# Linear layer's start placed ahead of the state space layer's tail, its norm weights applied to transposed features, and the windowed layers' dates changed

## Chip, cores and metric

One Trainium2 chip, one core. The metric is the device time of one execution in microseconds (us), as a median over runs; lower is better. A core has five engines that run their own instruction streams in order and wait for one another by semaphores: TensorE (PE, matmul and transpose, with weight loads shown as PEld), VectorE (DVE), ScalarE (ACT), GpSimd (POOL) and SyncE (SP, which issues most transfers). Matmul results land in PSUM, everything else lies in SBUF.

## What is computed

Four layers on x of 4 x 1024 tokens with 256 features, all fp32:

```python
x = x + mamba(_layernorm(x), ...)                 # state space layer, 16 states, 512 channels
x = x + experts(_layernorm(x), ...)               # 8 experts, the best one of each token
x = x + _L1_attn_ref(_layernorm(x), ...)          # linear attention and its own feed-forward
x = x + _L1_ffn_ref(_layernorm(x), ...)           # two layers of windowed attention and feed-forward

def _L1_attn_ref(x, wq, wk, wv, wo, proj, w1, b1, w2, b2, g1, beta1, g2, beta2):
    h = _ln(x, g1, beta1)                         # (x - mean) * rsqrt(var + 1e-5) * g1 + beta1
    q = _phi((h @ wq).reshape(b, s, H, DH), proj) # elu(q @ proj) + 1, 16 heads of 64
    k = _phi((h @ wk).reshape(b, s, H, DH), proj)
    v = (h @ wv).reshape(b, s, H, DH)
    ...                                           # causal: kv and ksum run over the tokens
    x = x + attn @ wo
    h2 = _ln(x, g2, beta2)
    return x + (gelu(h2 @ w1 + b1) @ w2 + b2)
```

Two norms follow one another at the linear layer: the plain one of the model and the layer's own, with weights g1 and beta1.

## The kernel before

`run()` calls three methods one after the other: `mamba` (state space layer and experts), `linear` and `local` (both windowed layers). Every instruction passes through one helper on line 98, so the profile shows L98 everywhere and instructions are told apart by their tiles. A scheduler decides the order on each engine: where `nc.hold` is set an instruction keeps its place in program order, elsewhere it is free to move. Tokens are worked in groups of 512 (`G` = 4 blocks of 128 partitions), eight in all.

`mamba` (line 271) has a main loop over 256 steps (subsequence and state), held in program order. Behind it `nc.hold` is off, and there follow the last `output` (transposes py and acc, summed in PSUM), `finish` (the gated product, po with w_out), the experts still left (`rest`) and the last subsequence's `experts`. An experts step normalizes, computes router logits (PE's pl), on POOL and DVE the weights of the chosen expert (lg, w, cw), transposes them on PE (pcw, from cw) and runs eight experts' products (pe, from w_e, high and low halves of each fp32 operand apart: names in h and l).

`linear` (line 838) opens its pools, loads the feature projection pj, and has these parts. `weights(o)` multiplies wq and wk by pj for eight heads (PE's pf from a tile raw that a DMA on SP's queue fills) and splits the result and wv into high (ACT) and low (DVE; POOL for wv). `norm(n)` loads group n's tokens z (group 0, z0, on POOL's queue) and applies the plain norm. `project(n)` runs `features`: statistics, rstd on POOL, then for each half of the group hn = (z - mean) * rs on DVE, times the row g1 and plus the row beta1 on POOL, four transposes on PE into PSUM (pt, tag p5, three buffers shared with pf), and a split of pt into hth (ACT) and htl (DVE). Then follow the projections pq and pv. `rows` holds g1, beta1 and b2 spread over all partitions by transfers on ACT's queue.

The streams `ahead` (project) and `behind` (forward, the feed-forward) are advanced step by step in a loop over units (group, half of the heads, block) with scores (pa, masked to am), values (po, at), turn (transposes to oth, otl) and add (pw with l_wo, added to z). What is left of `behind` goes to `local`, which runs it between the first windowed group's steps.

`local` (line 1233) places its steps by dates written out as constants: a place is 10 times a tile's number plus an offset. BEHIND holds the offsets of the linear layer's leftover steps, REST the point at which that layer's buffers are freed for the windowed layers' weights, EARLY, ELOAD, EPAIR, ETURN and HOLD the steps of the first groups, TABLES and W1G0 those of weights.

The part of `features` that the change touches:

```python
for name, op in affine:
    nc.gpsimd.tensor_tensor(
        hn, hn, rows[name].unsqueeze(1).to_broadcast([P, 2, D]), op
    )
yield
pt = ps.tile([P, 2, 2 * P], F32, tag="p5", name="pt")
```

Of the kernel before, what the change touches and what calls it, by code (L numbers as in the profile page):

```python
# [9 lines left out]
F32 = mybir.dt.float32  # L10
F32R = mybir.dt.float32r
AF = mybir.ActivationFunctionType
ALU = mybir.AluOpType
AX = mybir.AxisListType
PSUM = bass.MemoryType.PSUM
DRAM = bass.MemoryType.DRAM

P = 128
D = 256
NB = 4  # L20
# [3 lines left out]
G = 4  # L24
# [13 lines left out]
HP3 = H3 // 2  # L38
FF = 1024
NF = FF // P  # L40
VW = 65
# [83 lines left out]
class Kernel:  # L125
# [142 lines left out]

    def mamba(self, xs):

        tc, ins = self.tc, self.ins
        nc = self.nc
        T, NQ = 2 * P, 2
        NSUB = NB * L // T
        SEQ = L // T
        LATER = (7, 8, 9, 10, 11, 12, 13, 14, 15)
        with ExitStack() as es:
            def pool(name, bufs, **kw):  # L280
                return es.enter_context(tc.tile_pool(name=name, bufs=bufs, **kw))

            early = pool("m_a", 1)
            mid = pool("m_f", 1)
            wp = pool("m_w", 1)
            wk = pool("m", 1)
            dp = pool("m_d", 3, space=DRAM)

            ps_d = pool("m_pd", 1, space=PSUM)
            ps_h = pool("m_ph", 2, space=PSUM)  # L290
            ps = pool("m_ps", 3, space=PSUM)

            st = [{} for _ in range(NSUB)]

# [470 lines left out]
            for s in range(NSUB):  # L765
# [10 lines left out]
                if s > 0:  # L776
                    e = experts(s - 1)
# [23 lines left out]
            for k in range(K):  # L801
# [24 lines left out]
                        now()  # L826
                tokens_first(k)
            nc.hold = False
            for t in range(2):
                output(K - 1, t)  # L830
            run(finish(NSUB - 1))
# [6 lines left out]
    def linear(self, xs, ys):  # L838


        nc, tc, ins = self.nc, self.tc, self.ins
        late, kept = ExitStack(), ExitStack()
        with ExitStack() as es:
# [4 lines left out]

            wp = pool("l_w", 1)
            st = wf = pool("l_f", 1)  # L850


            wa = pool("l_a", 1)
            wo_ = pool("l_o", 1)
            wz = pool("l_z", 1, late, side="right")
            wb = pool("l_b", 1, late, side="right")
            wl = pool("l_w2", 1, late, side="right")
            ps = pool("l_ps", 3, kept, space=PSUM)
            ps_t = pool("l_pt", 1, space=PSUM)
            ps_a = pool("l_pa", 1, space=PSUM)  # L860
            ps_o = pool("l_po", 2, space=PSUM)

            NG = 2 * NB
            ctx = [{} for _ in range(NG)]
# [14 lines left out]
            def weights(o):  # L879
# [23 lines left out]
                    raw = self.raw(st, tag="e", bufs=2, src=ins["l_wv"][k * P : (k + 1) * P, at])  # L903
                    self.split(wv[:, k, at], raw, nc.gpsimd)


            keep = wz.tile([P, P], F32, name="keep")
            nc.gpsimd.memset(keep, 1.0)
            nc.gpsimd.affine_select(
                out=keep, in_=keep, compare_op=ALU.is_ge, fill=0.0, base=0,  # L910
                pattern=[[1, P]], channel_multiplier=-1,
            )

            kv = wz.tile([P, HP3, 2, VW], F32, name="kv")
            nc.gpsimd.memset(kv, 0.0)

            def features(pool, z, dst, affine=(), **kw):

                st_ = pool.tile([P, G, 6], F32, name="fst", bufs=2)
                mv = pool.tile([P, G, 2], F32, name="fmv", bufs=2)  # L920
                for t in range(G):
                    nc.vector.bn_stats(st_[:, t, :], z[:, t, :])
                    nc.vector.bn_aggr(mv[:, t, :], st_[:, t, :])
                rs = self.rstd(pool, mv, G)
                for t in range(0, G, 2):
                    hn = pool.tile([P, 2, D], F32, name="hn", **kw)
                    for j in range(2):
                        nc.vector.tensor_scalar(
                            hn[:, j, :], z[:, t + j, :], mv[:, t + j, 0:1], rs[:, t + j : t + j + 1],
                            ALU.subtract, ALU.mult,  # L930
                        )
                    for name, op in affine:
                        nc.gpsimd.tensor_tensor(
                            hn, hn, rows[name].unsqueeze(1).to_broadcast([P, 2, D]), op
                        )
                    yield
                    pt = ps.tile([P, 2, 2 * P], F32, tag="p5", name="pt")
                    for k in range(2):
                        for j in range(2):
                            nc.tensor.transpose(  # L940
                                pt[:, k, j * P : (j + 1) * P], hn[:, j, k * P : (k + 1) * P],
                                self.ident,
                            )
                    yield
                    self.split(dst[:, :, t * P : (t + 2) * P], pt)

            def split_tile(pool, name):
# [14 lines left out]
            def project(n):  # L962
                ht = split_tile(wf, "ht")
                yield from features(
                    wf, ctx[n]["z"], ht, (("g1", ALU.mult), ("beta1", ALU.add)), tag="e", bufs=2
                )
                for o in range(2):
                    if n == 0 and o == 1:
                        weights(1)
                    qt, kt, vs = [], [], []  # L970
                    ctx[n]["heads"].append((qt, kt, vs))
                    for hp in range(4):
                        at = slice((4 * o + hp) * P, (4 * o + hp + 1) * P)
                        for name, w, dst in (("q", wq, qt), ("k", wk_, kt)):
                            pq = ps.tile([P, GT], F32, tag="p5", name="pq")
                            self.mm3(pq, [(w[:, k, at], ht[:, k, :]) for k in range(2)])
                            yield

                            e = wf.tile([P, GT], F32, name="e", bufs=2)
                            nc.scalar.activation(e, pq, AF.Exp)  # L980
                            nc.vector.tensor_scalar(e, e, 1.0, None, ALU.min)
                            s = wa.tile([P, GT], F32, name=name + "t", bufs=7)
                            nc.vector.scalar_tensor_tensor(s, pq, 0.0, e, ALU.max, ALU.add)
                            dst.append(s)
                    for t in range(G):
                        tok = slice(t * P, (t + 1) * P)
                        pv = ps.tile([P, GT], F32, tag="p5", name="pv")
                        self.mm3(
                            pv,
                            [(ht[:, k, tok], wv[:, k, o * 512 : (o + 1) * 512]) for k in range(2)],  # L990
                        )
                        yield

                        v_ = wa.tile([P, 8, VW], F32, name="va", bufs=3)
                        nc.gpsimd.memset(v_[:, :, 64:65], 1.0)
                        nc.scalar.copy(v_[:, :, 0:64], pv.rearrange("p (h e) -> p h e", e=64))
                        vs.append(v_)
                if n + 1 < NG:
                    norm(n + 1)
                yield  # L1000
# [184 lines left out]
            def stream(f):  # L1185
                for n in range(NG):
                    yield from f(n)

            norm(0)
            weights(0)  # L1190
            rows = {n: self.row(wf, n, D) for n in ("g1", "beta1")}
            rows["b2"] = self.row(wz, "b2", D)
            ahead, behind = stream(project), stream(forward)
            made = [0, 0]
            count = 4 + NF + NF // 2 * (2) + 1

            def projected(unit):
# [28 lines left out]
                        if lag <= i < len(units) + lag:  # L1226
                            f(*units[i - lag])
            run(ahead)
        return behind, late, kept, ps

    def local(self, xs, behind, late, kept, ps):
# [3 lines left out]
        with kept, ExitStack() as es:  # L1237
# [129 lines left out]
            def w2_part(l, c):  # L1367
# [16 lines left out]
            ADD_LAST = (7, 12)  # L1384
            LOAD = (1, 10, 15, 16)
            FORWARD = (4, 5, 7, 7, 7, 9, 9, 19, 19, 21, 21, 21, 23, 25, 26, 29, 32, 36, 38, 39, 45, 46, 61)
            FIRST = (-6, 2, 5, 6, 6, 9, 14)
            LOAD_FIRST = (4, 10, 16, 17)
            W1G0 = (15, 20, 18, 19)
            W1V0 = (25, 30, 28, 31)  # L1390
            W20 = (37, 41, 44, 46, 47, 52)
            QKV = (4, 6, 7, 8, 11, 12)
# [1 line left out]
            W1G = (37, 39, 40, 45)  # L1394
            W1V = (45, 50, 55, 60)
            W2 = (57, 68, 74, 77, 78, 86)
            ELOAD, EPAIR, ETURN, REST, HOLD = (-62, -60, -60, -58), (-44, -16), (-29, -13), -5, -2
            TABLES, O0 = (-42, -24, 8, 23, 32, 39), (-2, 6, 6, 8)
            EARLY = (
                (-44, -42, -42, -36, -34, -33, -33),  # L1400
                (-39, -33, -28, -28, -28, -28, -21),
                (-29, -15, -15, -15, -12, -7, 2),
                (-20, -4, -4, -1, 4, 9, 13),
            )
            BEHIND = (
                -51, -50, -47, -47, -47, -46, -40, -37, -35, -31, -31, -30, -24, -24, -18, -15,
                -14, -13, -12, -7, -1, 5,
            )


# [475 lines left out]
    def run(self, phases=("mamba", "linear", "local")):  # L1886
        nc, tc = self.nc, self.tc
        with ExitStack() as es:
            cp = es.enter_context(tc.tile_pool(name="const", bufs=1))
            dp = es.enter_context(tc.tile_pool(name="dram", bufs=1, space=DRAM))  # L1890
            self.constants(cp)
            xs = [dp.tile([P, G, D], F32, name=f"xs{i}") for i in range(2 * NB)]
            if "mamba" in phases:
                self.mamba(xs)
            if "linear" in phases:
                ys = [dp.tile([P, G, D], F32, name=f"ls{i}") for i in range(2 * NB)]
                left = self.linear(xs, ys)
                xs = ys
            if phases[-1] == "local":
                self.local(xs, *left)  # L1900
            else:
# [109 lines left out]
```

## Time and profile before

| | value |
|---|---|
| runs | 3405.77, 3407.74, 3413.19 us; median 3407.74 |
| profiled execution, its own time | 3408.97 us |
| its span, granted clock | 3407.3 us, 0.968 |
| PE busy | 3105.7 us (91%) |
| DVE busy | 2590.5 us (76%) |
| ACT busy | 2050.5 us (60%) |
| POOL busy | 1939.0 us (57%) |
| instructions | 59830 |

Times in the profile count from the first instruction. The state space layer's loop ends near 1129; from there to 1236 its tail and the start of the linear layer overlap; the linear layer runs to about 2100, a seam to the windowed layers to about 2260, and those to the end at 3407. In a view by windows each engine has its busy time and, behind the x, the number of its instructions; PEclk is the granted TensorE clock as a share of full speed. In a list of waits "PE a <- POOL b" says that PE stood before an instruction writing a until POOL had made b. In an order of time the bracket gives the idle time of the engine just before, and what ended it.

### The profile page before, as it was taken

To read this page: it belongs to the slowest core of one execution; us is meant where nothing else is said; L and a number is where in the kernel's file an instruction comes from. 1 tells how busy PE (TensorE), PEld (TensorE's weight loads), DVE (VectorE), ACT (ScalarE), POOL (GpSimd) and SP (SyncE) were. 2 spreads that over 40 slices of the span, in tenths; PEclk is the share of its full clock that TensorE was granted. 3 is DMA by queue.
4 is the path that set the end of the run, shared out by engine and by line. 5 is a ranking of instruction groups with operands and counts; after the bars stand their busy time and mean duration, and the time that the engine had idled before them with its cause. 6 is when DMAs were issued, how large, how long until landed. Compare 5 with 4: busy or idle time off the path is not lost.

```text
span 3407.3 us, 59830 instructions
## 1 busy us (share of the span) xinstructions
PE 3105.7 (91%) x21872; PEld 2639.4 (77%) x21872; DVE 2590.5 (76%) x5796; ACT 2050.5 (60%) x4082; POOL 1939.0 (57%) x2301
## 2 busy tenths in 40 slices
PE   5788888888887899999999999899999999999998
PEld 4666667666766788898888888778888888888886
DVE  6899999999999576667766766677777677777663
ACT  7777777777775232433343434676666777666664
POOL 5988888888788321001101103677677766767671
PEclk8799999999999899999999999899999999999998
DMA  2011111111110110000000002211111111111111
GB/s 92 32 44 38 36 39 46 38 36 40 41 35 29 54 63 4 1 13 20 20 7 13 19 7 77 72 32 37 48 48 49 60 40 56 47 38 46 38 41 35
DMA packets 83973, 130.60 MB, mean 38 GB/s; under 512 B 10080, under 2 KB 58016, under 8 KB 83680
## 3 DMA queue, kind: packets, MB, share of 16 engines
q1 hardware_dynamic: 81216, 124.68, 11.4%
q8 instruction: 174, 2.85, 0.3%
q10 hardware_dynamic: 2320, 1.57, 0.2%
q14 instruction: 119, 0.97, 0.1%
q0 software_dynamic: 144, 0.52, 0.0%
HBM read 99.21 MB, written 27.53 MB: 37 GB/s over the span
## 4 chain that ended last, share of the span: by engine, by line
PE 63%; DVE 16%; POOL 7%; ACT 7%; issue 6%; DMA 1%; POOLq 0%; SPq 0%; DVEq 0%; ACTq 0%
PE pq L98 10%; PE pw L98 10%; PE po L98 8%; PE pa L98 7%; PE pt L98 6%; DVE hs L98 6%; POOL hs L98 3%; PE pe L98 3%; PE pf L98 3%; PE ph L98 3%; PE pp L98 2%; PE py L98 2%; PE pv L98 2%; ACT gl L98 2%; DVE acc L98 2%
## 5 line engine op out<-in xcount | busy, mean ns | idle before, releaser
L98 POOL TENSOR_TENSOR hs<-uc,bn 128x1024 f32<-128x1024 f32 x256 | 608.7, 2378 | 67.0 <-PE ph L98 53.3
L98 DVE TENSOR_TENSOR_SCAN hs<-da,hs 128x512 f32<-128x512 f32 x512 | 608.3, 1209 | 25.2 <-POOL hs L98 12.4
L98 PE MATMUL ph<-ident,hs 128*128 128x128 f32 x2048 | 336.7, 297 | 131.7 <-DVE hs L98 66.4
L98 ACT ACTIVATE da<-dt,a 128x510 f32<-128x510 f32 x512 | 346.8, 687 | 141.7 <-DVE hs L98 135.5
L98 PEld LDWEIGHTS ph<-ident,hs 128*128 128x128 f32 x2048 | 242.6, 149 | 225.6 <-DVE hs L98 78.1
L98 POOL MEMSET va<- 128x8 f32 x64 | 7.5, 120 | 578.5 <-PE pk L98 461.5
L98 POOL TENSOR_TENSOR u<-u,ro 128x512 f32<-128x512 f32 x128 | 175.5, 1371 | 246.0 <-DVE ro L98 199.4
L98 ACT ACTIVATE sm<-sm,mx 128x256 f32<-128x256 f32 (+1 forms) x512 | 248.5, 488 | 97.6 <-DVE mx L98 96.6
L98 PE MATMUL pq<-wqkvh,yt 128*128 128x512 f32 x768 | 287.0, 415 | 0.7 <-ACT yt L98 0.7
L98 POOL TENSOR_SCALAR sm<-sm,sums 128x256 f32<-128x256 f32 (+1 forms) x512 | 237.1, 481 | 81.1 <-DVE sums L98 75.8
L98 ACT ACT_TABLE_LOAD x146 | 187.3, 1283 | 59.7 <-DVE gl L98 31.9
L98 ACT ACTIVATE term<-ph,ct 128x512 f32<-128x512 f32 x288 | 181.4, 682 | 56.6 <-PE ph L98 56.5
L98 DVE CUSTOM_DVE_ANT_0 sm<-pp,band 128x256 f32<-128x256 f32 (+1 forms) x512 | 177.8, 403 | 42.6 <-PE pp L98 42.1
L98 POOL TENSOR_TENSOR ss<-ss,power 128x16 f32<-128x16 f32 x64 | 187.7, 2932 | 5.3
L98 ACT ACTIVATE e<-pq 128x512 f32<-128x512 f32 x128 | 75.8, 597 | 184.4 <-PE pq L98 172.9
L98 PEld LDWEIGHTS pq<-wqkvh,yt 128*128 128x128 f32 x768 | 144.3, 188 | 38.2 <-issue 9.6
L98 ACT ACTIVATE sq<-pq 128x512 f32<-128x512 f32 x128 | 76.6, 599 | 142.2 <-DVE ro L98 105.1
L98 DVE SCALAR_TENSOR_TENSOR acc<-ph,ct,acc 128x512 f32<-128x512 f32 x192 | 139.7, 728 | 17.4 <-PE ph L98 17.4
L98 PE MATMUL pq<-wqkvl,yt 128*128 128x512 f32 x384 | 152.0, 396 | 0.0
L98 PE MATMUL pa<-fh,w1h 128*128 128x512 f32 x320 | 134.3, 420 | 19.1 <-ACT v L98 15.7
L98 PE MATMUL py<-ident,term 128*128 128x128 f32 x1152 | 149.1, 279 | 0.0
L98 PE MATMUL po<-va,am 128*128 128x65 f32 x1024 | 146.8, 261 | 0.0
(325 smaller groups left out, 10252.7 us busy)
## 6 DMA issues: line engine op xcount, KB each, us to landing
bn<-bd SPq DMA_DIRECT2D x64, 512.0 KB
tab<-tab SPq DMA_DIRECT2D x64, 128.0 KB
line<-yg SPq DMA_DIRECT2D x64, 128.0 KB
hn<-line SPq DMA_DIRECT2D x64, 128.0 KB
xr<-in_x SPq DMA_DIRECT2D x16, 256.0 KB
xs<-xr SPq DMA_DIRECT2D x16, 256.0 KB
hn<-xs SPq DMA_DIRECT2D x16, 256.0 KB
ls<-hn SPq DMA_DIRECT2D x16, 256.0 KB
```

Of the source, the lines that this page charges most:

```text
L98: now = f(*args, **kw)
```

## The change

Three parts.

1. `mamba` takes the generator `linear`. Its pools m_a and m_pd (a PSUM pool) are closed behind the main loop, the others move to the other side of the memory, and then `linear` runs up to its first `yield`: pools l_w, l_f and l_ps, pj, the constant keep, the cleared sums kv, `norm(0)`, `weights(0)` and four steps of `project(0)`, which are both halves' normalization and transposes. In program order all this now lies ahead of the last `output`, `finish` and the experts. The other pools of `linear` are opened behind the `yield`.
2. The rows g1 and beta1 and the 32 POOL products with them are gone. The transposed features have one feature per partition, so weights are now two scalars per partition: 32 DVE instructions, two to each pt, in place in PSUM.
3. `local` has other dates.

```diff
-    def mamba(self, xs):
+    def mamba(self, xs, then):
...
+        first = ExitStack()
...
-            early = pool("m_a", 1)
-            mid = pool("m_f", 1)
-            wp = pool("m_w", 1)
-            wk = pool("m", 1)
+            early = pool("m_a", 1, first)
+            ps_d = pool("m_pd", 1, first, space=PSUM)
+            wk = pool("m", 1, side="right")
+            wp = pool("m_w", 1, side="right")
+            mid = pool("m_f", 1, side="right")
...
             nc.hold = False
+            first.close()
+            next(then)
             for t in range(2):
                 output(K - 1, t)
...
-                    for name, op in affine:
-                        nc.gpsimd.tensor_tensor(
-                            hn, hn, rows[name].unsqueeze(1).to_broadcast([P, 2, D]), op
-                        )
                     yield
...
+                    if affine:
+                        for k in range(2):
+                            nc.vector.tensor_scalar(
+                                pt[:, k, :], pt[:, k, :], self.v("g1", k), self.v("beta1", k),
+                                ALU.mult, ALU.add,
+                            )
                     self.split(dst[:, :, t * P : (t + 2) * P], pt)
...
             norm(0)
             weights(0)
-            rows = {n: self.row(wf, n, D) for n in ("g1", "beta1")}
-            rows["b2"] = self.row(wz, "b2", D)
+            rows = {}
             ahead, behind = stream(project), stream(forward)
             made = [0, 0]
+            for _ in range(4):
+                made[0] += 1
+                next(ahead)
+            yield
...
-            FIRST = (-6, 2, 5, 6, 6, 9, 14)
+            FIRST = (-5, 2, 3, 4, 6, 7, 14)
-            W1G0 = (15, 20, 18, 19)
+            W1G0 = (16, 22, 20, 19)
-            ELOAD, EPAIR, ETURN, REST, HOLD = (-62, -60, -60, -58), (-44, -16), (-29, -13), -5, -2
-            TABLES, O0 = (-42, -24, 8, 23, 32, 39), (-2, 6, 6, 8)
+            ELOAD, EPAIR, ETURN, REST, HOLD = (-68, -58, -56, -51), (-46, -20), (-23, -12), -10, -3
+            TABLES, O0 = (-41, -22, 11, 23, 34, 39), (-2, 6, 6, 8)
...
             BEHIND = (
-                -51, -50, -47, -47, -47, -46, -40, -37, -35, -31, -31, -30, -24, -24, -18, -15,
-                -14, -13, -12, -7, -1, 5,
+                -61, -60, -54, -54, -54, -52, -47, -42, -32, -31, -28, -26, -23, -22, -20, -18,
+                -15, -14, -12, -7, 6, 8,
             )
...
             xs = [dp.tile([P, G, D], F32, name=f"xs{i}") for i in range(2 * NB)]
+            ys = [dp.tile([P, G, D], F32, name=f"ls{i}") for i in range(2 * NB)]
+            linear = self.linear(xs, ys)
             if "mamba" in phases:
-                self.mamba(xs)
...
+                self.mamba(xs, linear)
```

The four lists of EARLY change as well, each offset by up to 5 places.

More of the change, by code (lines that the diff above doesn't have):

```diff
@@ L278, in mamba, with pool @@
         LATER = (7, 8, 9, 10, 11, 12, 13, 14, 15)
+        first = ExitStack()
         with ExitStack() as es:
-            def pool(name, bufs, **kw):
-                return es.enter_context(tc.tile_pool(name=name, bufs=bufs, **kw))
-            early = pool("m_a", 1)
-            mid = pool("m_f", 1)
-            wp = pool("m_w", 1)
-            wk = pool("m", 1)
+            def pool(name, bufs, to=es, **kw):
+                return to.enter_context(tc.tile_pool(name=name, bufs=bufs, **kw))
+            early = pool("m_a", 1, first)
[3 more added lines that the diff above has]
+            mid = pool("m_f", 1, side="right")
             dp = pool("m_d", 3, space=DRAM)
-            ps_d = pool("m_pd", 1, space=PSUM)
-            ps_h = pool("m_ph", 2, space=PSUM)
-            ps = pool("m_ps", 3, space=PSUM)
+            ps_h = pool("m_ph", 2, space=PSUM, side="right")
+            ps = pool("m_ps", 3, space=PSUM, side="right")
             st = [{} for _ in range(NSUB)]
@@ L850, in linear @@
             st = wf = pool("l_f", 1)
[L853 to L857, printed above, removed]
             ps = pool("l_ps", 3, kept, space=PSUM)
-            ps_t = pool("l_pt", 1, space=PSUM)
-            ps_a = pool("l_pa", 1, space=PSUM)
-            ps_o = pool("l_po", 2, space=PSUM)
             NG = 2 * NB
@@ L904, in weights, with features @@
                     self.split(wv[:, k, at], raw, nc.gpsimd)
[L907 to L911, printed above, removed]
-            )
-            kv = wz.tile([P, HP3, 2, VW], F32, name="kv")
-            nc.gpsimd.memset(kv, 0.0)
-            def features(pool, z, dst, affine=(), **kw):
+            def features(pool, z, dst, affine=False, **kw):
                 st_ = pool.tile([P, G, 6], F32, name="fst", bufs=2)
@@ L931, in features @@
                         )
-                    for name, op in affine:
-                        nc.gpsimd.tensor_tensor(
-                            hn, hn, rows[name].unsqueeze(1).to_broadcast([P, 2, D]), op
-                        )
                     yield
@@ L964, in project @@
                 yield from features(
-                    wf, ctx[n]["z"], ht, (("g1", ALU.mult), ("beta1", ALU.add)), tag="e", bufs=2
+                    wf, ctx[n]["z"], ht, affine=True, tag="e", bufs=2
                 )
@@ L1187, in stream @@
                     yield from f(n)
+            keep = wf.tile([P, P], F32, name="keep")
+            nc.gpsimd.memset(keep, 1.0)
+            nc.gpsimd.affine_select(
+                out=keep, in_=keep, compare_op=ALU.is_ge, fill=0.0, base=0,
+                pattern=[[1, P]], channel_multiplier=-1,
+            )
+            kv = wf.tile([P, HP3, 2, VW], F32, name="kv")
+            nc.gpsimd.memset(kv, 0.0)
             norm(0)
             weights(0)
-            rows = {n: self.row(wf, n, D) for n in ("g1", "beta1")}
-            rows["b2"] = self.row(wz, "b2", D)
+            rows = {}
             ahead, behind = stream(project), stream(forward)
             made = [0, 0]
+            for _ in range(4):
+                made[0] += 1
+                next(ahead)
+            yield
+            wa = pool("l_a", 1)
+            wo_ = pool("l_o", 1)
+            wz = pool("l_z", 1, late, side="right")
+            wb = pool("l_b", 1, late, side="right")
+            wl = pool("l_w2", 1, late, side="right")
+            ps_t = pool("l_pt", 1, space=PSUM)
+            ps_a = pool("l_pa", 1, space=PSUM)
+            ps_o = pool("l_po", 2, space=PSUM)
+            rows["b2"] = self.row(wz, "b2", D)
             count = 4 + NF + NF // 2 * (2) + 1
@@ L1228, in linear @@
             run(ahead)
-        return behind, late, kept, ps
+        yield behind, late, kept, ps
     def local(self, xs, behind, late, kept, ps):
@@ L1396, in local @@
             W2 = (57, 68, 74, 77, 78, 86)
-            ELOAD, EPAIR, ETURN, REST, HOLD = (-62, -60, -60, -58), (-44, -16), (-29, -13), -5, -2
-            TABLES, O0 = (-42, -24, 8, 23, 32, 39), (-2, 6, 6, 8)
+            ELOAD, EPAIR, ETURN, REST, HOLD = (-68, -58, -56, -51), (-46, -20), (-23, -12), -10, -3
+            TABLES, O0 = (-41, -22, 11, 23, 34, 39), (-2, 6, 6, 8)
             EARLY = (
[L1400 to L1403, printed above, removed]
+                (-45, -44, -43, -37, -37, -35, -33),
+                (-36, -35, -30, -26, -26, -26, -17),
+                (-34, -18, -15, -15, -11, -7, 4),
+                (-18, -7, -2, 1, 7, 12, 15),
             )
             BEHIND = (
-                -51, -50, -47, -47, -47, -46, -40, -37, -35, -31, -31, -30, -24, -24, -18, -15,
-                -14, -13, -12, -7, -1, 5,
+                -61, -60, -54, -54, -54, -52, -47, -42, -32, -31, -28, -26, -23, -22, -20, -18,
+                -15, -14, -12, -7, 6, 8,
             )
@@ L1892, in run @@
             xs = [dp.tile([P, G, D], F32, name=f"xs{i}") for i in range(2 * NB)]
+            ys = [dp.tile([P, G, D], F32, name=f"ls{i}") for i in range(2 * NB)]
+            linear = self.linear(xs, ys)
             if "mamba" in phases:
-                self.mamba(xs)
[L1895 to L1898, printed above, removed]
+                self.mamba(xs, linear)
+            else:
+                next(linear)
+            left = next(linear)
+            xs = ys
             if phases[-1] == "local":
```

## The prediction

> **What bounds the kernel now.** I read the page's totals first (PE 91% busy, granted clock 0.968), then windows by stage, then TensorE's (PE's) list of waits in the worst one, then the order of time on the engine it waits for. Busy time by stage, in us (x instructions), then granted clock, DMA share and GB/s:
>
> ```profile
> 1129.00:1236.00 107.00, 94.49 (x564) 80.00 (x563) 70.60 (x198) 30.67 (x61) 40.09 (x55) 0.92 0.28 90
> 1236.00:2100.00 864.00, 849.93 (x6178) 760.95 (x6178) 580.85 (x1452) 325.71 (x511) 114.67 (x160) 0.99 0.05 16
> 2100.00:2260.00 160.00, 142.34 (x1007) 117.99 (x1006) 112.00 (x332) 94.30 (x245) 112.79 (x133) 0.93 0.19 56
> ```
>
> The columns are PE, PE weight loads, VectorE (DVE), ScalarE (ACT), GpSimd (POOL). From 1236 to 2100, nearly all of the linear layer, PE is busy 98% at clock 0.99: only PE's own work sets the time there. The change can win in two places, the seam between state space layer and linear layer (PE idle 12.5 us of 107) and the one to the windowed layers (17.7 of 160). PE's waits in the first (sum, times, longest):
>
> ```profile
> PE pcw L98 <- POOL cw L98: 6.8, 1, 6.8
> PE pf L98 <- DVE wql L98: 2.5, 1, 2.5
> PE pq L98 <- DVE qt L98: 1.4, 1, 1.4
> PE pf L98 <- DMA raw<-in_l_wk: 1.2, 1, 1.2
> ```
>
> The large one is the last router: POOL makes the expert weights cw, PE transposes them (pcw) and only then may the last expert matmuls (pe) go. Start, duration, instruction, idle time before; POOL, then PE, then windows of 4 us:
>
> ```profile
> 1156.68 1.27 POOL L98 TENSOR_TENSOR wvl<-raw,wvh 128x512 fp32r<-128x512 f32 x1 [5.45 <-ACT wvh L98]
> 1158.41 1.26 POOL L98 TENSOR_TENSOR wvl<-raw,wvh 128x512 fp32r<-128x512 f32 x1 [0.46 <-ACT wvh L98]
> ...
> 1161.77 1.05 POOL L98 TENSOR_SCALAR cw<-hit,m,w 128x8 f32<-128x8 f32 x2 [0.50 <-DVE m L98]
> 1162.80 2.48 POOL L98 TENSOR_TENSOR hn<-hn,r_g 128x512 f32<-128x512 f32 x2
> 1165.24 2.50 POOL L98 TENSOR_TENSOR hn<-hn,r_beta 128x512 f32<-128x512 f32 x2
> ```
>
> ```profile
> 1162.88 0.38 PE L98 MATMUL pcw<-ident,cw 128*16 128x128 f32 x1 [6.78 <-POOL cw L98]
> ...
> 1167.08 0.63 PE L98 MATMUL pe<-w_eh,eth 128*128 128x512 f32 x1
> 1167.51 0.63 PE L98 MATMUL pe<-w_el,eth 128*128 128x512 f32 x1
> ```
>
> ```profile
> 1164.00:1168.00 4.00, 4.00 (x10) 2.68 (x10) 0.69 (x1) 0.00 (x0) 3.74 (x4) 0.50 0.00 0
> ```
>
> POOL is in order, so the router stands behind two weight splits that waited for DMA. The norm's two row products follow, so the first transposes of hn come only at 1172.34: PE had no work of the linear layer to put into the gap. The gap costs twice. After it the clock is 0.50 and pe starts are .427 apart (1167.08 to 1167.51) instead of the .233 seen at full clock; 12 of them lose 12 x .194 = 2.3 us. The slow transposes around it and a second such spell at 1208 (clock 0.57, 16 pf in 3.31 against about 1.9) add some 2.5. So all idle and slow clock of this seam is 12.5 + 2.3 + 2.5 = about 17.
>
> **The change part by part.**
>
> *Early start.* Beside the windows the instruction orders of both kernels are used. In the new order the first weight-projection matmuls (pf) move from behind the last experts' first batch into the last output transposes (four at a time, from PE's index 5370, about 1132), hn's eight transposes lie before the router, and 24 pq matmuls (hth times wq, wk) stand directly before pcw, with 16 more in front of the router's logits. The moved steps also issue early two loads for pj, one load each for z0 and pieces of wq, wk, wv on their queues. z0 is 512 KB, lands 4.0 us after issue before, and is issued some 10 us earlier; wq's loads still wait for the same slots. Walking in order with durations of before: pf from 1132.6, w_out's product 1139.6 (+2.5), hn 1147.4 to 1148.5 (its second half behind a wv split, 1.27), transposes 1147.9 to 1150, the new DVE instructions to 1153.9, ACT's hth 1154.5, DVE's htl 1155.6. Here PE runs dry for about 2. The router takes some 4.4 us from logits to cw in POOL, DVE and PE; 24 pq x .23 = 5.5 cover it, so the 6.8 goes, and with it the 2.3 of clock. If the cover is not ready, up to 6.8 + 2.3 returns.
>
> What is late next: DVE. Norm work of the next three groups, weight splits and first scores all fall between 1196 and 1212, where DVE already shows 4.00 busy in 4 us in four windows running. I find PE waits of .5 (wk's second load), 1.1, 1.3, 3.4 (values behind weight splits on ACT), 1.9 (otl), 1.3 (am), 1.1 and .6, with the 2 above 13.2 in all, but mostly short ones. The first addition of the linear layer's output, same work before it in both orders, comes at 1235.8 before and in my walk at about 1227: 8.8 us. A walk with a slower matmul pitch gave 2.5; all idle gone is 17. I take 8.8, range 2 to 17.
>
> *Weights of the norm.* Removed: two row loads on ACT's queue and 32 POOL products, each about 1.27 (2.48 and 2.50 for two). POOL is busy 115 of 864, and PE's waits from 1236 to 2100 name no POOL tile: worth 0 there. Added: 32 DVE multiply-adds of 128x256 in PSUM. Before has none that writes PSUM; nearest rows:
>
> ```profile
> L98 DVE TENSOR_TENSOR z<-z,pw 128x256 f32<-128x256 f32 x64 | 26.8, 419 | 35.8 <-PE pw L98 35.5
> L98 DVE TENSOR_SCALAR gl<-pf,l_b 128x512 f32<-128x512 f32 x32 | 23.8, 745 | 8.5 <-PE pf L98 8.0
> L98 DVE TENSOR_SCALAR yg<-yg,mv,rs 128x256 f32<-128x256 f32 x4 | 1.5, 408 | 0.0
> ```
>
> Mean ns is the number behind the comma. From .37 (half of gl) to .745 (its whole); .42 by the row of the same size that reads PSUM: 32 x .42 = 13.4, and 28 of them, 11.8, within 1236 to 2100, where DVE goes from 581 to 593 of 864. DVE stays covered by PE. What is not free is the chain: the pair holds one of three PSUM buffers .84 longer, and ACT's hi copy, then DVE's lo, come that much later, 14 times. PE's work on other heads covers it; without that cover 14 x .84 = 11.8. POOL's .24-to-1.1 rstd stays. I take +1.5 (0 to 11.8).
>
> The Trainium skill, "VectorE: DVE Perf Modes", on PSUM operands, says that fp32 runs double rate from SBUF alone and single rate once any operand is in PSUM, which speaks against this move. The rows above are .408 for SBUF alone and .419 with PSUM, so little of it shows at this size; by the rule an affine costs up to twice the SBUF row, some .8, 26 us of DVE in all, and an estimated chain cost of 14 x 1.6 = 22 if uncovered.
>
> *Windowed layers' plan.* Only dates change: remaining forward steps of the linear layer (BEHIND) and the first groups' steps (EARLY, ELOAD, FIRST) go earlier by a few places. At this seam POOL decides one wait:
>
> ```profile
> 2154.06 1.90 POOL L98 TENSOR_TENSOR u<-u,ss 128x1024 f32<-128x1024 f32 x1
> 2155.92 1.27 POOL L98 TENSOR_TENSOR u<-u,ro 128x512 f32<-128x512 f32 x1
> ...
> 2160.09 1.67 POOL L98 TENSOR_SCALAR sm<-sm,sums 128x128 f32<-128x128 f32 x4
> ```
>
> PE's wait for that sm is 3.18 at 2160.66. In the new order the 1.27 product, and a later 2.92 power, go out of the second and third sm's way: about 2 each at most; half is given back to q and k made later. I take -3 (-8 to +4; the lower end is half of 17.7 idle, the upper one such pow and one product back in front).
>
> **Sum.** -8.8 + 1.5 - 3 = -10.3. The profiled execution took 3408.97 (span 3407.3), 1.2 over the median of 3407.74; so 3398.7 for such an execution, 3397.4 for the median.
>
> **Rivals.**
> 1. *DVE takes over.* For: four full windows from 1196 to 1212; the new order adds more to them. Against: what moves away before 1165 leaves DVE room (busy 2.4 of 4 or less there). The router's 9 shrinks to 3: -3 + 1.5 - 2 = -3.5, 3404.
> 2. *Everything packs.* For: gaps shorter than PE's lost 6.8 keep the clock at 1.00 as in 1144 to 1156. Against: single waits above must all vanish. -17 + 0 - 6 = -23, 3385.
> 3. *Slower: the affine chain in PSUM.* For: DVE is in order, with qt, kt, am of .69 each queued in front of each affine, and the buffers it holds are also those of pf and pt. Against: PE waits for hth or htl nowhere from 1236 to 2100. A cost per transposed half of .84 plus one queued .69 is 1.53 x 14 = 21; the sum is -8.8 + 21 - 3 = +9, 3417. It decides once a half costs above 11.8 / 14 = .84.
> 4. *Nothing moves:* the scheduler put the steps there already. The orders speak against it; 3408.
>
> The Trainium skill, "TensorE: Matmul & The Clock Gate", on the clock gate, puts the drop after about 3.4 us of idling. Here clock 0.50 follows the idle 6.78 and none follows 1.4; by that rule the new 3.4 wait could cost an estimated extra 2.
>
> **Chances.** Forecast .56, rival 1 .12, rival 2 .15, rival 3 .15, rival 4 .02. The point is the forecast's, 3397.5. Range 3385 to 3413: it begins at rival 2's time and ends 4 short of rival 3's, so about half of each (.07 and .08) is left out. 0.2% (6.8 us) is what a measurement here tells from no change. Faster: .48 of the forecast and rival 2, .63; same: .08 of it, rival 1 less .01, rival 4, .21; slower: rival 3 and .01, .16.
>
> **What would show it.** PE's wait pcw on cw below 1 and no clock near 0.5 around 1165; first addition into z near 1227; hn transposes near 1148. Affine rows near 420 ns; PE still idle about 14 in the linear layer; no PE wait on htl there. If that idle grows by 10 or the first addition is not before 1233, I am wrong; so too if the wait for sm at the second seam is replaced by one as long.

## The result: slower, and the profile after

The changed kernel takes 3417.10 us (median of 13 runs, 3412.01 to 3423.17), the kernel of before 3408.96 us (13 runs on the same chip). The ratio is 1.0022 with a 95% interval of 1.0015 to 1.0030: 8 us slower where 10 faster were forecast. The profiled execution has a span of 3413.0 us, 5.7 more than before.

The windows by stage of the changed kernel, same columns as before (PE, weight loads, DVE, ACT, POOL, granted clock, DMA):

```profile
1129.00:1236.00 107.00, 93.65 (x550) 78.20 (x549) 72.51 (x192) 30.75 (x59) 32.14 (x47) 0.93 0.29 88
1236.00:2100.00 864.00, 848.54 (x6170) 758.60 (x6170) 589.38 (x1483) 325.75 (x510) 71.89 (x126) 0.99 0.04 14
```

The first stage still has 13 us of idle PE and got through fewer of PE's instructions (550 for 564), although the router's wait of 6.8 is gone. What replaced it stands in PE's list of waits from 1196 to 1250 of the changed kernel; in before this stretch has two waits, 2.5 for wql and 1.4 for qt:

```profile
PE pb L98 <- DVE l_b L98: 2.7, 1, 2.7
PE pq L98 <- DVE qt L98: 2.4, 1, 2.4
PE pa L98 <- DVE am L98: 2.2, 2, 1.3
PE pt L98 <- DVE otl L98: 1.6, 1, 1.6
```

All four name DVE, but before the two longest DVE itself stood waiting for ACT's exponentials e:

```profile
1204.86 1.00 DVE L98 TENSOR_SCALAR e<-e 128x512 f32<-128x512 f32 x1 [3.72 <-ACT e L98]
...
1236.23 0.63 DVE L98 TENSOR_SCALAR e<-e 128x512 f32<-128x512 f32 x1 [4.18 <-ACT e L98]
```

At the first place ACT takes e behind copies of wvh and l_woh, at the second behind a copy of l_w2h whose load had come late. The other two waits (am, otl) fall where DVE is full. The windows of 4 us of the changed kernel:

```profile
1208.00:1212.00 4.00, 2.73 (x19) 2.00 (x17) 3.96 (x14) 1.98 (x4) 0.73 (x1) 0.50 0.70 227
...
1224.00:1228.00 4.00, 2.22 (x22) 1.82 (x23) 4.00 (x11) 0.41 (x1) 0.73 (x1) 1.00 0.16 50
...
1232.00:1236.00 4.00, 2.30 (x12) 2.21 (x11) 0.05 (x1) 1.11 (x3) 3.35 (x6) 0.50 0.37 118
...
1240.00:1244.00 4.00, 4.00 (x21) 4.00 (x21) 0.93 (x4) 0.00 (x0) 0.00 (x0) 0.50 0.00 0
```

From 1208 to 1232 DVE (third busy time) is full in all six windows, PE (first) is hollow in five of them, POOL (fifth) is under 1 in four. By the trace's record the clock stands at 0.50 twice: from 1207.4 to 1217.7, behind the wait for qt and before DVE is full, and from 1231.3 to 1248.4, the last 8 us of it with PE busy all the while. What DVE does in between, by groups, 1204 to 1236 of the changed kernel:

```profile
L98 DVE BATCH_NORM_STATS2 st<-z 128x6 f32<-128x256 f32 x12 | 4.3, 411 | 0.9 <-DMA z<-xs 0.9
L98 DVE TENSOR_SCALAR z<-z,mv,rs 128x256 f32<-128x256 f32 x8 | 3.7, 511 | 0.0
L98 DVE SCALAR_TENSOR_TENSOR l_w1l<-raw,vecs,l_w1h 128x512 fp32r<-128x512 f32 x4 | 2.9, 731 | 0.0
```

It is the plain norm's statistics of the next three groups, whose loads come in together, its application to two of them (1218.6 to 1223.4; the third group's comes at 1333), and weight splits, between the score work that PE waits for.

To see where time went, the same PE instruction was looked up in both traces. The table gives the median shift against before in us at four places (end of the main loop, time 1277 of before, 2015, 2315), the difference of the spans, and the time at half clock in the first seam (1128 to 1262), the linear layer's interior (to 2090) and the second seam (to 2290), each of one profiled execution. Such an execution can lie off its median: that of w2_pool is the slowest of its 11 (3418.24), that of start_alone 8.4 above its median, that of affine_alone 4.4 below.

```
kernel             loop   1277   2015   2315    end | half clock: seam  interior  seam 2
before              0.0    0.0    0.0    0.0    0.0 |       20.5      13.6    23.9
changed             2.3    9.7    6.5    6.6    5.7 |       27.3       3.4    10.2
start_alone        -0.4    5.8    5.0   15.7   16.5 |       37.5       6.8    40.9
affine_alone        0.9    3.7   -0.3   -0.5    2.0 |       27.2       3.4    20.5
dates_alone         3.8    1.4   -1.0   -1.5   -1.4 |       17.1       6.8    17.0
no_dates            0.6    5.5    4.7   11.9   11.2 |       17.0       6.8    34.1
w2_pool             4.1    9.8    9.5   10.5    9.2 |       27.3      10.2    20.4
pairs               2.5    4.2    1.1    1.3    3.4 |       20.4       3.4    20.4
before_pairs        1.2    5.8    3.0    6.9    8.8 |       27.3      10.2    30.7
z_pool             -0.6   -6.0  -20.7  -16.8  -15.1 |        6.8       6.8    20.4
pairs_z_pool        3.3   -1.8  -16.4  -12.8  -12.5 |       13.6       6.8    20.4
z_pool_seam         4.3    3.1   -0.5    0.9   -0.6 |       13.6       6.8    20.4
before_z_pool       2.3   -0.8  -19.4  -15.5  -13.4 |       20.5       0.0    23.9
z_pool_no_start    -0.6   -5.6  -20.4  -19.5  -16.9 |       13.6       0.0    17.0
```

In the changed kernel the first seam costs 9.7 - 2.3 = 7.4. At 1200 it is still ahead of before, by 5 to 7 us (an estimate: PE's instructions done by then, each at its pace at full clock), so all is lost between 1200 and 1250. From 1200 to 1252 PE is idle for 10.3 us in the changed kernel and for 4.0 in before, and the clock is at half for 27.3 and 6.8. The interior gives back 3.2. The shift at the loop's end is scatter of single executions, and dates_alone, whose orders up to 2090 are nearly before's, shows -2.4 in the seam and -2.4 in the interior: below 3 us the table tells nothing, and the medians decide.

### The profile page after: what moved, and what is told of

Same layout as the page of the kernel before. It is cut to its first block, busy times and chain, and to the rows that moved or that the text cites. A ratio compares the mean times of both kernels' runs of the same rounds, so it can differ in the third digit from the quotient of the medians.

```text
span 3413.0 us, 59827 instructions
## 1 busy us (share of the span) xinstructions
PE 3104.1 (91%) x21872; PEld 2632.3 (77%) x21872; DVE 2605.5 (76%) x5828; ACT 2056.5 (60%) x4082; POOL 1906.4 (56%) x2269
## 4 chain that ended last, share of the span: by engine, by line
PE 61%; DVE 14%; POOL 9%; ACT 7%; issue 6%; DMA 2%; SPq 0%; POOLq 0%; DVEq 0%; ACTq 0%
PE pw L98 10%; PE pq L98 10%; PE po L98 7%; PE pa L98 7%; PE pt L98 6%; DVE hs L98 5%; POOL hs L98 4%; PE pv L98 3%; PE pf L98 3%; PE pe L98 3%; PE ph L98 2%; PE pp L98 2%; PE py L98 2%; ACT gl L98 2%; DVE acc L98 2%
## 5 line engine op out<-in xcount | busy, mean ns | idle before, releaser
L98 POOL TENSOR_TENSOR hs<-uc,bn 128x1024 f32<-128x1024 f32 x256 | 616.2, 2408 | 65.6 <-PE ph L98 51.8
```

Of the source, the lines that this page charges most:

```text
L98: now = f(*args, **kw)
```

## The experiments

Times are medians against before on the same chip, ratios with their 95% interval.

**The three parts.** *start_alone* is the changed kernel with rows g1 and beta1 applied by POOL and before's dates.

```diff
-                    if affine:
-                        for k in range(2):
-                            nc.vector.tensor_scalar(pt[:, k, :], pt[:, k, :], ...)
+                    for name, op in affine:
+                        nc.gpsimd.tensor_tensor(hn, hn, rows[name]..., op)
```

> The early start alone: norm weights stay rows that POOL applies, the windowed layers' dates stay those of before. Theory A (late weight loads at the seam: ACT stands in order at casts l_w2h whose loads come late, PE starves and loses its clock around 1205 to 1250): most of the change's loss is here, +3 to +12 us against before, with PE clock near 0.5 somewhere between 1200 and 1250. Theory B (the affine in PSUM costs the time): the early start by itself gains, -5 to -10 us. Theory C (the new dates cost it): also -5 to -10 us here.

3417.09 against 3408.15, ratio 1.0027 (1.0017 to 1.0037): +9. Its clock is 0.50 from 1209 to 1243. The early start loses; the forecast's gain isn't there even without the other parts. With before's dates it loses 10.7 more between 2015 and 2315 in its profiled execution.

*affine_alone* is before with the norm weights as in the changed kernel.

> The norm weights alone move to transposed features (32 DVE multiply-adds in PSUM in place of 32 POOL products and two row loads); start and dates as before. Theory A: no loss in the linear layer's interior, PE idle from 1236 to 2100 within 3 us of the 14 before, whole time -6 to +3 us. Theory B: +6 us or more, with that idle up by 6 or more.

3415.44 against 3408.15, ratio 1.0011 (1.0001 to 1.0020). The medians are 7.3 apart, the ratio says +4; either is beyond the first theory's bound of +3. The table has no loss in the interior (3.7 to -0.3), where PE is idle for 12.9 us from 1236 to 2100 (14.1 in before), but one of 2.8 in the seam, about the scatter: with POOL's row products gone, the scheduler starts the linear layer early by itself (18 pq matmuls before pcw, last pe 60.4 us after the loop, as with the early start; 54.4 before). So theory B, which asked for more idle time in the interior, is out, and the parts are not independent.

*dates_alone* is before with the new constants, *no_dates* the changed kernel with the old ones.

> Only the windowed layers' dates are changed. Theory A: -4 to +3 us, all of it after 2100. Theory C: +6 us or more, after 2100.

> The changed kernel with before's dates for the windowed layers. The seam at 1200 as in the changed kernel. If the new dates only follow the early start: the second seam, 2100 to 2260, loses 5 to 10 us, the whole is 5 to 10 above the changed kernel. If the dates are worth nothing: within 3 us of it.

dates_alone: 3406.45 against 3408.15, ratio 0.9994 (0.9985 to 1.0003), no difference. no_dates: 3420.23 against 3410.27, ratio 1.0034 (1.0021 to 1.0048), 1.2 parts in a thousand, 4 us, above the changed kernel's ratio, and +7.2 from 2015 to 2315 where the changed kernel has +0.1. So the dates seem to be worth something only behind the early start; it isn't clear of the noise, since the intervals of no_dates and of the changed kernel overlap.

**Is it ACT behind late weight loads?** In the changed kernel, DVE stands 4.18 us before 1236 for ACT's exponentials e, which are queued on ACT behind eight l_w2h copies whose loads land 3.3 us apart. *w2_pool* puts those copies on POOL:

```diff
+                if hi:
+                    hi.tensor_copy(w[:, c, at].hi, raw)
+                    self.nc.gpsimd.tensor_tensor(w[:, c, at].lo, raw, w[:, c, at].hi, ALU.subtract)
+                    continue
                 self.split(w[:, c, at], raw, self.nc.gpsimd)
...
-                    w2 = self.split_weights(wl, wb, "l_w2", ins["l_w2"], NF, D, tag="gl", bufs=5)
+                    w2 = self.split_weights(wl, wb, "l_w2", ins["l_w2"], NF, D, hi=nc.gpsimd, tag="gl", bufs=5)
```

> The changed kernel with the eight high copies of l_w2 on POOL in place of ACT, so that ACT's feature exponentials (e) stand behind no load of l_w2. Theory A: 5 to 10 us below the changed kernel, so -2 to +3 against before, PE clock at 1.00 from 1225 to 1250, ACT e no longer ends an idle time of 4 us on DVE there. Theories B and C: as the changed kernel, +6 to +10 against before.

3412.29 against 3408.15, ratio 1.0011 (1.0002 to 1.0019): about half of the loss is gone, less than theory A asked for. Its windows of 4 us:

```profile
1224.00:1228.00 4.00, 2.22 (x13) 1.60 (x13) 4.00 (x11) 0.00 (x0) 1.35 (x2) 1.00 0.13 38
...
1240.00:1244.00 4.00, 4.00 (x20) 4.00 (x21) 0.92 (x4) 0.00 (x0) 0.72 (x1) 0.50 0.02 9
```

ACT (fourth busy time) is now idle, PE is as hollow as it was, DVE is full, and the half clock still follows. Theory A in this form is a part at most: PE's wait for l_b is gone, and there, at 1237, PE's instructions, in the same order as in the changed kernel, gain 2.8 us on it; the hollows before stay. The next form (A2) came from a number: from the last expert result to the first output product pw there are 51.3 us in before, 50.9 in the changed kernel and 51.5 in affine_alone, as if one chain of loads set it. *pairs* shortens that chain, with 4 loads of two chunks each for l_wo and l_w2:

```diff
-                raw = self.raw(stage, src[c * P : (c + 1) * P, at], **kw)
-                self.split(w[:, c, at], raw, self.nc.gpsimd)
+            raw = stage.tile([P, 2, width], F32, name="raw", **kw)
+            self.nc.sync.dma_start(raw, src[c * P : (c + 2) * P, :].rearrange("(c p) d -> p c d", p=P))
+            self.split(w[:, c : c + 2, :], raw, self.nc.gpsimd)
```

> The changed kernel with l_wo and l_w2 loaded and split two chunks at a time: 4 loads of 256 KB each instead of 8 of 128 KB. Theory A2 (the seam is a chain from the end of the last experts through the load queue, where each l_w2 load waits for the split of the one before, and through ACT in order; 51 us from the last expert result to the first output product pw in before, changed and affine_alone alike): the l_w2 chain of 8 x 3.3 us becomes 4 x about 4, the 51 falls to 36 to 46, the whole time to 3 to 10 us below the changed kernel. Theory D (DVE's norm of three groups at once sets the seam): at most 2 us.

> The kernel of before with l_wo and l_w2 in pairs. There PE is busy through most of the same 51 us (5 idle), so by theory A2 little can be won: -4 to +1. If it wins as much as it does on the changed kernel (over 4), the loads were no cost of the change in particular.

pairs: 3414.51 against 3409.10, ratio 1.0012 (1.0004 to 1.0021), some 3 us better than the changed kernel's ratio, with the 51 at 45.9: A2's least. before_pairs: 3415.80, ratio 1.0022 (1.0012 to 1.0031), slower by 7, which neither theory expected; there the 51 grew to 59.2. The loads are at most one link, not the bound, and the equal 51 was no sign of one chain.

**Is it DVE?** *z_pool* moves the application of the plain norm, z = (z - mean) * rs, to POOL for groups 1 to 7, *z_pool_seam* for groups 1 to 3, *pairs_z_pool* adds the pairs, *before_z_pool* does it to before, and *z_pool_no_start* to affine_alone with the new dates:

```diff
-                self.layernorm(wz if n else wf, [z], [z], G)
+                self.layernorm(wz if n else wf, [z], [z], G, engine="p" if n else "v")
```

> The changed kernel with the plain norm of groups 1 to 7 applied on POOL in place of DVE (28 instructions of 128x256, 0.45 us each on DVE, 12 of them in the seam: 5.4 us). Theory D: 3 to 6 us below the changed kernel, the 51 from the last expert result to the first pw falls by as much. Theory A2: within 3 us of the changed kernel, the 51 stays above 48.

> Both: loads in pairs and the plain norm of groups 1 to 7 on POOL. Theory A2: as loads in pairs alone, or 2 us better. Theory D: as the norm on POOL alone. If the two are links in series behind one another: 6 to 12 us below the changed kernel, so -4 to +2 against before.

z_pool: 3393.90 against 3409.10, ratio 0.9960 (0.9947 to 0.9972), 21 us below the changed kernel's ratio where theory D had 3 to 6. pairs_z_pool: 0.9963 (0.9950 to 0.9975), no better. So the norm's place on DVE costs time, and more than theory D gave the seam. The expectation counts 12 of the 28 instructions in the seam; in the traces 8 lie there, and 20 in the interior.

> The changed kernel with the plain norm of groups 1 to 3 alone on POOL, that of groups 4 to 7 on DVE as it was. Theory D: the seam is as with all groups on POOL (first pw about 39 us after the last expert result, half clock there 7 to 14 us), the interior as in the changed kernel; 10 to 16 us below the changed kernel. If the gain lay in the interior (half-clock spells there gone): under 5 us below the changed kernel.

3406.46 against 3410.27, ratio 0.9985 (0.9976 to 0.9994): 12 instructions of about 0.4 us each on DVE, 8 of them in the seam, moved to POOL take about 13 us off the changed kernel (1.0022 - 0.9985), and its loss is gone. The first pw comes 41.6 after the last expert result. PE's waits in 1196 to 1250, and two windows:

```profile
PE pq L98 <- ACT va L98: 3.0, 1, 3.0
PE pa L98 <- DVE am L98: 1.9, 2, 0.9
PE pq L98 <- DVE qt L98: 1.6, 1, 1.6
```

```profile
1212.00:1216.00 4.00, 1.03 (x7) 0.82 (x6) 3.97 (x14) 2.62 (x5) 2.52 (x5) 1.00 0.50 180
1216.00:1220.00 4.00, 4.00 (x26) 3.44 (x25) 3.92 (x11) 2.23 (x5) 4.00 (x5) 1.00 0.02 4
```

DVE is still full, but POOL (fifth busy time) now works beside it, PE is better fed from 1216 on, and half clock falls from 27.3 to 13.6. The window from 1212 is as hollow as any of the changed kernel, and no half clock follows it at once.

Up to 1247 of the changed kernel PE runs the same instructions in the same order in both, so another order of PE is no rival here. Between the same two of them, at 1219 and 1242 of the changed kernel, z_pool_seam gains 6.4 us on it; the first of the moved instructions starts at 1218.6 there. Another 2.5 it gains between 1202 and 1219, where the changed kernel's first spell of half clock has no counterpart. The moved instructions come too late to have done that, so it is the scatter of the clock, or another cause that stays open.

> The kernel of before with the plain norm of groups 1 to 7 on POOL, nothing of the change. If DVE's norm of three groups sets the seam whatever stands before it: 10 to 18 us below before, as on the changed kernel. If the change is what made DVE the bound (its affine and its early start): -5 to +2 us.

> Norm weights on transposed features, the new dates and the plain norm of groups 1 to 7 on POOL, without the early start. If the early start is worth what the forecast gave it once DVE is out of the way: 6 to 10 us above the same with the early start (3394). If it is worth nothing: within 3 us of it.

before_z_pool: 3395.33 against 3410.27, ratio 0.9954 (0.9941 to 0.9966). Nothing of the change is in it. Its seam is about before's (-0.8 - 2.3 = -3 at 1277, first pw 52.9 after the last expert result, half clock 20.5 there); its gain lies in the interior. Windows from 1262 to 2070, the first line of before, the second of before_z_pool:

```profile
1262.00:2070.00 808.00, 796.72 (x5801) 712.99 (x5799) 544.81 (x1357) 311.13 (x485) 102.79 (x145) 0.99 0.05 15
```

```profile
1262.00:2070.00 808.00, 807.58 (x5930) 724.23 (x5929) 553.53 (x1372) 316.73 (x496) 129.40 (x170) 1.00 0.06 18
```

Idle PE goes from 11.3 to 0.4, the clock to 1.00, and PE gets through 129 more instructions in the same 808 us. How the move does this is not shown. PE's longest waits of before in that stretch are

```profile
PE pw L98 <- ACT gh L98: 4.9, 4, 1.8
PE pa L98 <- DVE am L98: 2.2, 3, 0.9
```

Waits that name ACT make 5.6 of the 11.3, those that name DVE 5.4, and half clock sets in at 1563 and 1796, each time 1.2 us behind the end of a wait of 1.8 for ACT's gh. The scheduler also gives PE another order in before_z_pool, both there and in the seam, so a freer DVE and a better order are not told apart. z_pool_no_start is the fastest of all: 3391.28, ratio 0.9942 (0.9929 to 0.9954). It is not above z_pool (3393.90), so putting the linear layer's start ahead in the program buys nothing with DVE out of the way either: the scheduler does most of it by itself there (last pe 60.3 after the loop).

## Why the prediction was wrong

- *Early start, the router's wait and its clock.* The mechanism was right: no wait of pcw on cw is left and the clock is 1.00 around 1165. The transposes of hn came at 1152.3 for 1148, with the loop's end 2.3 late in this execution.
- *"What is late next: DVE"* is the step that failed. The place was named (four full windows from 1196 to 1212) and then priced by short waits, 13.2 in all, for -8.8. Measured is +7.4. (The 1235.8 that the prediction calls the first addition is the start of before's first output products pw, at 1235.66; the addition itself is at 1238.48. In the changed kernel they come at 1243.42 and 1246.36, so 8 later, not 8.8 earlier.) The order of work accounts for it: PE's linear work that was moved ahead of the experts made them end 5.8 us later after the loop (60.2 for 54.4) and was gone when the norms of three groups, whose loads follow the experts, came to DVE, which was full for 24 us. In before the same bunch met a PE with projections in stock: 35 pq and 24 pv matmuls lie between the last pe and 1200 there, none in the changed kernel, where all of them are done before the last pe. That this stock is what covered DVE in before is read from the orders; that the norm on DVE costs the changed kernel's seam is what z_pool_seam shows. Late experts alone are not the price: in z_pool_seam they end as late (61.9) and its seam is at -1.2. Nor is the norm on DVE the whole of it: the waits for ACT's e, behind weight copies whose loads came late, have a part, by w2_pool up to 2.8.
- *The clock.* The forecast took off the spell behind the router and put none behind the waits that were left; an extra 2 stood only beside the sum. No wait of the changed kernel from 1196 to 1250 is longer than 2.7, and still all 27.3 us of the seam's half clock lie there. Before had shown as much: its spell at 1208 follows a wait of 2.5. The Trainium skill, "TensorE: Matmul & The Clock Gate", Part 1 on the clock gate, puts the drop after an idle window of about 3.4 us; shorter hollows were enough here, so the measurement decides.
- *Weights of the norm.* The affine costs more than taken: mean ns of the new group in the changed kernel, 1129 to 2100:

```profile
L98 DVE TENSOR_SCALAR pt<-pt,vecs 128x256 f32<-128x256 f32 x32 | 17.3, 545 | 0.5
```

  545 ns for 420, 17.3 us for 13.4, inside the bounds given. No cost of the chain (+1.5) shows: the interior got 3 to 4 us shorter in affine_alone and the changed kernel, about the scatter, with 3.4 of half clock for 13.6. Rival 3 is out. That the measured 3417 is the very time it named is coincidence: it put the loss into the interior, and the loss lies in the seam.
- *"Only PE's own work sets the time there"*, of the interior, was wrong. before_z_pool takes 28 instructions of about 0.4 us, 20 of them in the interior, from a DVE that is busy 67%, and the interior falls by 19 us. So what runs on DVE, though covered on average, mattered there, by its own waits or through the order that it led to.
- *Windowed layers' plan.* Forecast -3, measured 0 (6.5 at 2015, 6.6 at 2315). The wait for sm fell from 5.2 to 3.6 as worked out; a new one took its place in the changed kernel's second seam (in before 2.2):

```profile
PE pw L98 <- DVE otl L98: 5.9, 3, 3.2
PE pt L98 <- POOL sm L98: 3.6, 4, 1.8
```

- *The rivals.* Rival 1, DVE takes over, had the mechanism. It let 3 of the seam's gain stand, because it counted only the busy time added to DVE, not PE work taken from under it. Its price was mis-sized: +7.4 for -3.

What is open: why before_pairs loses 7 us, how the norm on DVE costs the interior 11 to 19 us (z_pool against the changed kernel, before_z_pool against before), and how much of the seam's 7.4 would be left without the half clock. The amounts are known (6.3 us more idle, 20.5 us more at half clock between 1200 and 1252), but half clock follows on waits in every run, so no run shows one without the other.

## What to carry to other kernels

Work pulled forward into a gap is taken from a later place: ask which engine was covered by it there, and whether it is full in that window, whatever its mean over the stage says. A small move off an engine that is full in bursts (12 instructions of some 0.4 us) was worth more than the removal of the longest wait in the list. When a list says that PE waited for DVE, see what DVE waited for just before. Where waits are short but frequent, look at the granted clock behind them before pricing them at their own length.

## What was not expected of the hardware

Time at half clock comes in steps of about 3.4 us (3.4, 6.8, 10.2, 13.7, 17.1, 34.1 in the traces), and which of these a given hollow leads to differs between executions of nearly the same order: in the first seam 20.5 us in before and 17.1 in dates_alone. A wait of 2.4 led to half clock in the changed kernel, one of 3.0 in z_pool_seam did not at once. In the interior, before has four such steps (13.6 us), none with PE idle for more than 1.8 at a time just before it; with 11 us less idle time there are none.
